# Decoder layer: the normalised tokens of the later batches rounded in two pairs, context queries rounded later, feed-forward seams rearranged

## The chip, the cores and the metric

The kernel runs as one program on one core of a Trainium2 chip. The core has a matrix engine (PE in the profile, with its weight loads as PEld), a vector engine (DVE), a scalar engine (ACT), GpSimd (POOL) and SP, which here only issues DMAs. Each engine takes its own instructions strictly in the order in which the program gives them, and waits where an operand is not there yet. The metric is the device time of one execution in microseconds, lower is better, as the median of several runs.

## The reference

One decoder layer over `x` of 8 batches, 112 tokens, 512 features, with a context of 375 tokens for each batch:

```python
x = x + attention(layernorm(x), Wqkv, Wqkv_b)              # 16 heads of 32, rotary, causal
# second attention, on l = _ln(layernorm(x), ln_w, ln_b):
q  = (_div_clamp_fp8(l, q_in_scale)  * q_in_scale)  @ wq   # and k, v with scales of their own
qx = (_div_clamp_fp8(l, qx_in_scale) * qx_in_scale) @ wqx  # queries of the context
core = gqa(ln(q), ln(k), v); xout = gqa(ln(qx), ln(kx), vx)  # kx, vx from ctx_2048
x = x + _div_clamp_fp8(concat(core, xout), proj_smooth) @ wproj * scale
# feed-forward with ternary weights
x = x + rms_norm(silu(gate) * up) @ ternary(w_proj),  gate, up = layernorm(x) @ ternary(w_gate_up)
```

`_div_clamp_fp8` divides by a scale, clips to 448 and rounds to an 8-bit float. The same normalised tokens are rounded four times, with four scales: m = 0 for q, 1 for k, 2 for v, 3 for the context's queries.

## The kernel before

The program is a hand-written order: the Python text runs once, and every call appends instructions to the engines' queues in that order. What is said here of order is therefore order on each engine. The stages, with their place in the profiled execution of before:

- **First attention.** Batches 0 to 3, then their transition, then batches 4 to 7 (from about 114 us). `batch(b, ...)` issues, for a pipeline of three batches, `values(b)`, `attended(b-2)`, `scores(b)`, `turned(b-1)` and `softmaxed(b)`. `joined` adds the result to `xb[b]` on POOL (L611), takes the statistics of `xb[b-1]` and normalises `xb[b-2]` on DVE (L161).
- **Rounding (`quantise`).** A group is a column block k of 128 features of four batches, that is 448 tokens. `quantise_turn` transposes it on PE (L332). `quantise_begin` scales it on ACT (L350) and takes |y| on ACT (L203). `round_a` clips both on DVE (L207, L208) and adds them on POOL (L210). The last subtraction writes `xq[m]` (L368), on POOL for batches 0 to 3 with m < 3, else on DVE. There are 8 groups and 4 values of m, so 32 such tiles, all 448 wide. The 16 tiles of batches 0 to 3 are begun beside first attention, and those of batches 4 to 7 only in the units that follow, by `quantise((4, 5, 3, 1, 1, 1, 1)[u.i])` after unit 0, 1, 2 and so on; m = 3 comes last.
- **Weights.** `split_chunk(s, what, k)` splits a weight chunk into two parts on ACT (L309) and DVE (L310); what = 0 is q's weights, 1 keys' and values', 2 the output's. The tiles for the parts come from a `Ring` of pools A, B and C; `load_raw` issues the next chunk's DMA on SP. The chunks (0, 0, k) and (0, 1, k) of the first head group are split after first attention.
- **Own units** 0 to 31 (from 164.2 us): four head groups s, in each 7 token tiles of 128 and one more step. `Own.project` makes q (8 matmuls at L691, 512 wide), then keys and values, statistics on DVE (L173, L174), and between them it calls `advance(stage, g)`, which lets earlier units take their next stage: normalising, transposing (`turn`, whose keys go through DVE at L833), scores, softmax, output. Unit i reads token tile i mod 8, so unit 3 is the first that needs tokens of batch 4.
- **Context units** 32 to 63 (from about 460 us) do the same against the context, with `xq[3]` as input of their queries.
- **Seam to the feed-forward** (about 1078 to 1122 us): the dictionary `between` puts `ffn_input(0)` (normalise four tiles, transpose, split), four `hidden_part` calls for the first 512 tokens and the last units' stages one after the other; `ffn_input(1)` for the other 384 tokens follows.
- **Feed-forward**: `hidden_part` multiplies by gate and up, `down` multiplies back. In the last `down` the row norm `rstd` comes from PE, DVE and POOL (L133), and then DVE does two operations for each of 7 tiles (L1414, L1415) before its DMA goes out.

## Time and profile before

| | us |
|---|---|
| median of 3 runs (lowest, highest) | 1285.07 (1284.45, 1289.41) |
| the profiled execution's own time | 1283.86 |
| its span, first to last instruction | 1282.1 |
| PE busy in the span | 1200.6 (94%) |
| DVE, ACT, POOL busy | 931.8, 815.8, 846.1 |
| first attention's batches 4 to 7, 116.0 to 164.2 | 48.2; DVE busy 46.56 |
| own units 0 to 3, 164.2 to 214.2 | 50.0; DVE busy 39.18, PE busy 33.89 |
| eight own units in the steady part, 317.34 to 384.64 | 67.3; DVE busy 56.42, PE busy 62.77 |
| seam, 1078.0 to 1122.2 | 44.2; PE busy 36.08 |

The profile is one execution. Busy time is the union of an engine's instructions; matmul ends are modelled, so a busy PE is not a PE at its peak. A group of instructions is told by line, engine and tile (output, then inputs), with its count, busy time, mean time of one and the idle time in front of it. In a timeline the two first columns are the start and the length, and a bracket gives the idle time before the instruction and the one whose end released it. "PEclk" is the clock that the matrix engine was granted, as a share of full speed.

### The profile page before, as it was taken

To read this page: it belongs to the slowest core of one execution; us is meant where nothing else is said; L and a number is where in the kernel's file an instruction comes from. 1 tells how busy PE (TensorE), PEld (TensorE's weight loads), DVE (VectorE), ACT (ScalarE), POOL (GpSimd) and SP (SyncE) were. 2 spreads that over 40 slices of the span, in tenths; PEclk is the share of its full clock that TensorE was granted. 3 is DMA by queue.
4 is the path that set the end of the run, shared out by engine and by line. 5 is a ranking of instruction groups with operands and counts; after the bars stand their busy time and mean duration, and the time that the engine had idled before them with its cause. 6 is when DMAs were issued, how large, how long until landed. Compare 5 with 4: busy or idle time off the path is not lost. (4 is left out here: it accounts for less than half of the span.)

```text
span 1282.1 us, 19634 instructions
## 1 busy us (share of the span) xinstructions
PE 1200.6 (94%) x6326; PEld 962.4 (75%) x6326; DVE 931.8 (73%) x2366; ACT 815.8 (64%) x2008; POOL 846.1 (66%) x938
## 2 busy tenths in 40 slices
PE   8997976889999889999999999999999998899998
PEld 5673765777888767888788778788777786687876
DVE  6647986887888866677776776677777775579864
ACT  2334676878687757667667767777667665456432
POOL 6657866687877756765767656667566655477762
PEclk9988886999999999999999999999999999999999
DMA  5001120213332354455554455554544440133201
GB/s 172 1 1 42 34 91 17 83 50 106 131 127 93 122 209 152 147 201 194 182 174 151 151 171 174 162 170 161 174 150 148 167 157 5 34 107 104 73 29 58
DMA packets 55511, 149.85 MB, mean 117 GB/s; under 512 B 6400, under 2 KB 15744, under 8 KB 55408
## 3 DMA queue, kind: packets, MB, share of 16 engines
q1 hardware_dynamic: 55408, 148.59, 35.3%
q8 instruction: 50, 0.82, 0.3%
q14 instruction: 53, 0.43, 0.1%
HBM read 120.18 MB, written 26.56 MB: 114 GB/s over the span
## 5 line engine op out<-in xcount | busy, mean ns | idle before, releaser
L912 PE MATMUL pa<-wx,ct 128*125 128x512 f32 x1152 | 289.4, 400 | 2.4 <-ACT wx L293 1.5
L912 PEld LDWEIGHTS pa<-wx,ct 128*125 128x125 f32 x1152 | 208.9, 186 | 51.2 <-ACT wx L293 1.9
L210 POOL TENSOR_TENSOR f8t<-y,big 128x512 f32<-128x512 bf16 (+1 forms) x88 | 107.4, 1224 | 140.2 <-DVE big L208 139.8
L738 POOL TENSOR_TENSOR p<-p,ri 112x448 f32<-112x448 f32 (+1 forms) x64 | 118.1, 1846 | 35.6 <-DVE ri L736 35.4
L923 DVE TENSOR_TENSOR kv<-kv,pa 125x512 f32<-125x512 f32 x96 | 65.9, 687 | 98.7 <-PE pa L912 52.2
L691 PE MATMUL pa<-hi,xq 128*128 128x512 f32 (+2 forms) x352 | 112.9, 345 | 11.0 <-DVE xq L368 9.2
L997 ACT ACTIVATE p<-ps,cmx 112x375 f32<-112x375 f32 x128 | 71.8, 574 | 75.5 <-DVE cmx L996 75.5
L1256 PE MATMUL pa<-h3T,wf 128*128 128x512 f32 (+1 forms) x512 | 110.0, 371 | 2.7 <-DVE sg L1266 2.7
L691 PE MATMUL pa<-lo,xq 128*128 128x512 f32 (+2 forms) x352 | 107.5, 331 | 0.9 <-DVE lo L310 0.9
L1256 PEld LDWEIGHTS pa<-h3T,wf 128*128 128x128 f32 x512 | 92.9, 188 | 14.9 <-DVE sg L1266 3.6
L174 DVE BATCH_NORM_AGGREGATE mv<-bst 128x2 f32<-128x6 f32 (+1 forms) x472 | 86.0, 182 | 16.3
L691 PE MATMUL ps<-hi,cq 128*128 128x512 f32 x224 | 90.8, 405 | 2.8 <-POOL cq L758 1.1
L730 ACT ACTIVATE qT<-ps,hln 128x448 f32<-128x448 f32 (+6 forms) x112 | 57.4, 567 | 56.1 <-PE ps L725 55.8
L691 PE MATMUL ps<-lo,cq 128*128 128x512 f32 x224 | 88.4, 395 | 0.0
L173 DVE BATCH_NORM_STATS2 bst<-pa 128x6 f32<-128x128 f32 x280 | 76.2, 272 | 16.2 <-PE pa L691 16.2
L988 PE MATMUL ps<-kT,qT 128*112 128x375 f32 x256 | 86.0, 478 | 0.5 <-ACT kT L974 0.5
L1158 POOL TENSOR_TENSOR th<-th,tw 128x512 bf16<-128x512 bf16 x48 | 59.1, 1231 | 40.1 <-DVE th L1150 40.1
L193 ACT ACTIVATE kv<-kv,ckvnm,ckvr 125x128 f32<-125x128 f32 x192 | 77.5, 491 | 6.2 <-POOL ckvnm L189 5.5
L691 PEld LDWEIGHTS pa<-hi,xq 128*128 128x128 f32 (+1 forms) x352 | 67.9, 193 | 17.3 <-DVE xq L368 10.7
L1021 PE MATMUL ps<-pT,kv 125*128 125x224 f32 x384 | 78.0, 353 | 0.0
L1021 PEld LDWEIGHTS ps<-pT,kv 125*128 125x128 f32 x384 | 72.6, 190 | 2.0
L691 PEld LDWEIGHTS pa<-lo,xq 128*128 128x128 f32 (+1 forms) x352 | 68.0, 193 | 7.4 <-DVE lo L310 3.8
(181 smaller groups left out, 3131.1 us busy)
## 6 DMA issues: line engine op xcount, KB each, us to landing
ct<-forms SPq DMA_DIRECT2D x84, 750.0 KB, 4.4
w<-in_wattn SPq DMA_DIRECT2D x96, 256.0 KB, 3.1
forms<-form SPq DMA_DIRECT2D x12, 750.0 KB, 4.7
forms<-ct SPq DMA_DIRECT2D x12, 750.0 KB, 5.1
tr<-in_wgu SPq DMA_DIRECT2D x32, 256.0 KB, 4.5
done<-th SPq DMA_DIRECT2D x48, 128.0 KB, 4.3
wh<-done SPq DMA_DIRECT2D x24, 256.0 KB, 3.7
tr<-in_wdown SPq DMA_DIRECT2D x16, 256.0 KB, 4.4
```

The lines of the kernel that those rows point to most:

```text
L173: nc.vector.bn_stats(st[: self.rows], a)
L174: nc.vector.bn_aggr(self.mv[: self.rows, self.at, :], st[: self.rows])
L193: nc.scalar.activation(dst, src, AF.Identity, bias=self.nm[:rows, i : i + 1], scale=self.r[:rows, i : i + 1])
L210: nc.gpsimd.tensor_tensor(t, y16, big, ALU.add)
L691: nc.tensor.matmul(out_, lhsT=lhsT, rhs=part[:, cut], start=first and i == 0, stop=last and i == 1)
L738: nc.gpsimd.tensor_tensor(u.p, u.p, bc, ALU.mult)
L912: nc.tensor.matmul(banks[bank][:CJ, :], lhsT=ct[:, at : at + CJ] if ct.dtype == F32R else ct[:, at : at + CJ].bitcast(F32R), rhs=split[sel ...
L923: nc.vector.tensor_tensor(kv, kv, banks[1][:CJ, :], ALU.add)
L988: nc.tensor.matmul(pp[:S, :SC], lhsT=qT[:, j, :], rhs=self.kT[:, j // 2, :], start=True, stop=True,)
L997: nc.scalar.activation(self.p[:, j, :], pp[:S, :SC], AF.Exp, bias=nm[:S], accum_out=self.sums[:S, j : j + 1])
L1021: nc.tensor.matmul(po[:, cut], lhsT=self.kv[j][:, 256 + g * P : 256 + (g + 1) * P], rhs=self.pT[:, j, cut], start=(j == 0), stop=(j == NJ ...
L1256: nc.tensor.matmul(pp[:, :n], lhsT=wcur[k][:, m * 256 + blk * P : m * 256 + (blk + 1) * P], rhs=hT[half, k][i], start=(k == 0 and i == 0), ...
```

## The change

- `qgroups` becomes (0, 1, 2, 3), (4, 5), (6, 7) by four values of k: the later batches are rounded in pairs, in tiles 224 wide. Each group has three rounded tiles (m = 0, 1, 2), 36 in all; for m = 3 only the scaled values are written to `xq[3]`, unrounded.
- `quantise` clips and subtracts one tile earlier than before, and now runs between batches, beside `batch(8)` and `batch(9)`, and, through `spot(i, n)`, at four places inside units 0 to 2 instead of after units.
- `round_q3` rounds `xq[3]` one token tile (128 partitions x 4 x 128) at a time inside units 5, 7, 9, 12, 14, 16 and 19.
- `joined` is only the addition; `normed` has the statistics (half 0) and the normalising (half 1).
- Pool `a1` moves to the other side of the memory, so that the weights' pool and ring B can open when the projections of first attention end; six of the first eight chunks are split inside the loop over batches 4 to 7, the other two beside `batch(8)` and `batch(9)`. Ring A has 16 tiles and A2 8 in place of 24.
- Seam: `ffn_input` is cut into `input_norms`, `input_turns` and `input_splits`, which are put between the last units' stages; the transposes go to `pa` banks (for the second half two `ps` and two `pa`).
- Last `down`: for tiles 3 to 6 the first of DVE's two operations becomes a scaling on ACT and an addition on POOL.

```diff
-    qgroups = [(0, k, (0, 1, 2, 3)) for k in range(KC)] + [(1, k, (0, 1, 2)) for k in range(KC)]
-    qgroups += [(1, k, (3,)) for k in range(KC)]
+    qgroups = [(bs, k) for bs in ((0, 1, 2, 3), (4, 5), (6, 7)) for k in range(KC)]
+    qtiles = [(i, m) for i in range(len(qgroups)) for m in range(3)]
...
+        scaled(y, i, m)
         qstate["y", t] = round_begin(y, s0, 6)
+        if m == 2:
+            k, cols = tokens_of(i)
+            scaled(xq[3][:, k, cols], i, 3)
...
-            if t < qstate["begun"] - (3 if begin else 0):
+            if t < qstate["begun"] - (2 if begin else 0):
...
-                engine = nc.vector if half or m == 3 else nc.gpsimd
+                engine = nc.vector if i >= KC else nc.gpsimd
...
+    def round_q3(b, step):
+        y = xq[3][:, :, b * P : (b + 1) * P]
+        if step == 0:
+            big = w2.tile([P, KC, P], BF, tag="f8m", name=uid("big"))
+            nc.scalar.activation(big, y, AF.Abs, scale=2.0**20)
+            q3state[b] = big
+        elif step == 1:
+            big = q3state[b]
+            nc.vector.tensor_scalar(y, y, 448.0, -448.0, ALU.min, ALU.max)
+            nc.vector.tensor_scalar(big, big, 448.0 * 2.0**20, 1.5 * 2.0**14, ALU.min, ALU.max)
+            t = w2.tile([P, KC, P], F32, tag="f8t", name=uid("f8t"))
+            nc.gpsimd.tensor_tensor(t, y, big, ALU.add)
+            q3state[b] = t, big
+        else:
+            nc.vector.tensor_tensor(y, *q3state.pop(b), ALU.subtract)
...
         for b in range(HB, B):
-            batch(b, B, 4 if b < B - 1 else 0)
-            quantise(4, False)
+            batch(b, B, 3 if b < B - 1 else 0)
+            quantise(3, False)
             if b >= HB + 2:
-                joined(b - 2, HB, B)
+                normed(b - 2)
+            for what, k in {HB: (), HB + 1: ((0, 0), (0, 1)), HB + 2: ((0, 2), (0, 3)), HB + 3: ((1, 0), (1, 1))}[b]:
+                split_chunk(0, what, k)
...
+    batch(B, B)
+    quantise(3, False)
+    split_chunk(0, 1, 2)
+    normed(B - 2, 0)
+    quantise(2)
+    normed(B - 2, 1)
+    to_tiles(B - 2)
+    quantise(2)
+    batch(B + 1, B)
+    split_chunk(0, 1, 3)
+    normed(B - 1, 0)
+    quantise(2)
+    normed(B - 1, 1)
+    quantise(2)
+    to_tiles(B - 1)
...
+    begins = {0: (1, 1, 1, 1), 1: (2, 2, 2, 2), 2: (2, 2, 0, 0)}
+    rounds = dict(zip((5, 7, 9, 12, 14, 16, 19), range(NT)))
+    def spot(i, n):
+        if i in begins:
+            quantise(begins[i][n])
+            if i == 2 and n > 1:
+                quantise(4, False)
+        elif i in rounds and n != 1:
+            round_q3(rounds[i], (0, None, 1, 2)[n])
...
-        if u.i < 7:
-            quantise((4, 5, 3, 1, 1, 1, 1)[u.i])
-        if u.i in (2, 7, 8):
-            quantise(5 if u.i == 2 else 3, False)
...
+    input_norms(0, 1)
+    last(1, "normed", "weigh")
+    input_norms(2, 3)
+    last(1, "out")
+    input_turns(0, 0, 1, 2, 3)
+    last(1, "turn_p", "attend", "turn", "rounded")
+    input_splits(0)
+    last(1, "score")
+    hidden_part(0, 0, 0)
+    last(2, "weigh")
+    hidden_part(0, 1, 0)
+    last(2, "turn_p", "out", "attend")
+    input_norms(4, 5)
+    last(2, "rounded")
+    hidden_part(1, 0, 0)
+    input_turns(1, 4, 5)
+    last(3, "out")
+    input_norms(6)
+    hidden_part(1, 1, 0)
...
+                for i in range(3, NT):
+                    nc.scalar.activation(ys[i], ys[i], AF.Copy, scale=rstd[:, i : i + 1])
+                    nc.gpsimd.tensor_tensor(ys[i], ys[i], xs[i], ALU.add)
...
-                nc.vector.scalar_tensor_tensor(ys[i], ys[i], r, xs[i], ALU.mult, ALU.add)
+                if i < 3:
+                    nc.vector.scalar_tensor_tensor(ys[i], ys[i], r, xs[i], ALU.mult, ALU.add)
```

`spot(i, 0)` stands after q's statistics of unit i, 1 before its keys and values, 2 after `advance("attend")` and before `advance("turn")`, 3 at the unit's end. `last(n, ...)` runs the named stages for the units that are left.

## The prediction

> **What bounds the kernel now.** I read the page first, then PE's busy time in short stretches, then what PE waited for, then the places where it waited, in order of time. The page says that PE is busy 94% of the span:
>
> ```profile
> PE 1200.6 (94%) x6326; PEld 962.4 (75%) x6326; DVE 931.8 (73%) x2366; ACT 815.8 (64%) x2008; POOL 846.1 (66%) x938
> ```
>
> So PE bounds the kernel, and what this change can win is PE's 81.5 us of idle time, or part of it. Busy time per stretch (columns: stretch, its length, then busy time and count for PE, PEld, DVE, ACT, POOL, then granted clock, DMA share, GB/s) shows the worst place:
>
> ```profile
> 184.00:188.00 4.00, 2.75 (x25) 2.53 (x23) 2.91 (x6) 2.52 (x5) 3.75 (x4) 1.00 0.00 0
> 188.00:192.00 4.00, 0.74 (x3) 0.41 (x3) 3.86 (x14) 3.61 (x8) 2.55 (x2) 0.91 0.00 0
> 192.00:196.00 4.00, 3.96 (x13) 2.54 (x12) 2.62 (x11) 4.00 (x15) 2.85 (x5) 0.50 0.00 0
> 196.00:200.00 4.00, 0.00 (x0) 0.00 (x0) 2.03 (x7) 1.13 (x3) 4.00 (x4) 0.50 0.00 0
> 200.00:204.00 4.00, 1.22 (x2) 0.50 (x2) 4.00 (x6) 3.94 (x10) 2.76 (x3) 0.50 0.00 0
> 204.00:208.00 4.00, 1.59 (x6) 1.38 (x7) 4.00 (x7) 0.46 (x2) 2.56 (x2) 0.50 0.00 0
> ```
>
> Of these 24 us PE is idle 13.74 (24 minus the sum of its column). That is unit 3, and the list of PE's waits names the tile, the rounded tokens of batches 4 to 7 that are not written yet (columns: total us, times, longest):
>
> ```profile
> PE pa L691 <- DVE xq L368: 9.2, 2, 6.1
> PE ps L332 <- DVE h L161: 6.8, 5, 3.2
> PE ps L725 <- ACT q L193: 4.5, 1, 4.5
> ```
>
> What makes the rounding late is DVE. In 116.0 to 214.2 (batches 4 to 7 and units 0 to 3) it is busy 46.56 + 39.18 = 85.7 of 98.2 us, 87%. Its groups there, by shape:
>
> ```profile
> L207 DVE TENSOR_SCALAR y<-y 128x448 bf16<-128x448 bf16 x28 | 16.1, 574 | 0.8 <-ACT big L203 0.8
> L208 DVE TENSOR_SCALAR big<-big 128x448 bf16<-128x448 bf16 x28 | 11.8, 421 | 0.0
> L368 DVE TENSOR_TENSOR xq<-f8t,big 128x448 fp32r<-128x448 f32 x12 | 10.7, 904 | 3.1 <-POOL f8t L210 3.1
> L368 DVE TENSOR_TENSOR xq<-f8t,big 128x448 bf16<-128x448 f32 x4 | 3.3, 825 | 0.0
> ```
>
> The reader is to see that 27.9 + 14.0 = 41.9 us, half of DVE's work there, is rounding. The other two places are the seam to the feed-forward, where PE's order shows its waits in brackets, and the tail:
>
> ```profile
> 1082.77 1.56 PE L1009 MATMUL ps<-ident,p 112*125 112x112 f32 x12 [2.54 <-POOL p L738]
> 1091.79 2.96 PE L1227 MATMUL ps<-ident,h 128*128 128x128 f32 x16 [1.14 <-ACT p L997]
> 1112.66 0.50 PE L691 MATMUL ps<-hi,cq 128*128 128x512 f32 x1 [1.12 <-POOL cq L758]
> 1120.03 0.30 PE L1227 MATMUL ps<-ident,h 128*128 128x128 f32 x1 [1.64 <-DVE h L161]
> ...
> 1266.70 9.58 PE L1389 MATMUL ps<-wf,hid 128*128 128x512 f32 x40
> 1267.12 1.52 POOL L133 TENSOR_TENSOR rms<-rms,expo 128x7 f32<-128x7 f32 x1 [2.25 <-DVE rms L1409]
> 1278.47 0.75 DVE L1415 SCALAR_TENSOR_TENSOR y<-ps,rms,y 128x512 f32<-128x512 f32 x1
> ```
>
> At the end PE is done at 1276.28 and DVE at 1279.22, so the last 3 us are DVE's.
>
> **Part 1, the rounding up to unit 4.** Before, 28 tiles are clipped in the stretch (0.574 + 0.421 = 0.995 us each) and 16 subtracted on DVE, 41.9 us. After, 12 tiles of 448 (11.9 us of clips, their subtraction on POOL, no m = 3) and 24 tiles of 224. The trace has no 224-wide rounding. Its two bounds are half of a 448 tile, (0.995 + 0.904) / 2 = 0.95 us, and a whole one, 1.90. I take half, because the nearest narrow row is near it: DVE's 112x256 multiplication at L547 takes 0.424 us where the 448-wide one at L508 takes 0.625, and without POOL at work the clips at 182.60 and 182.78 take 0.27. So 11.9 + 24 x 0.95 = 34.7 us, 7.2 less; with whole tiles 57.5 us, 15.6 more.
>
> The six weight chunks that move into the loop cost DVE the same as before (2.7 + 3.3 us at L310 for all eight, in this stretch in both kernels), and ACT 2.6 + 3.3 us. Their 13 loads go to SP earlier, ahead of the copies of x to its tiles; these are first read by the output of unit 5, over 30 us later, and the DMA share in 120 to 160 is under 0.2, so I cost them at nothing; without that cover a load costs the 3.1 us that it takes to land.
>
> `normed(4)` and `normed(5)` now stand in the loop: DVE's L161 waits for two small POOL instructions (0.25 and 0.55 us) queued behind up to three additions and three subtractions, 3 x (1.167 + 1.081) = 6.7 us at worst. Behind L161 on DVE stand the chunk splits and the next batch's values, on which PE waits. The row for it is 0.7 us (the one such wait in this stretch). I do not price it alone: I keep DVE's busy share at 87%, which leaves 11.5 us for waits of this kind.
>
> ACT gains the narrow tiles: 12 x 1.30 + 24 x 0.65 and eleven to twelve unrounded scalings of 0.36 to 0.72 make some 37 us where 31.2 were, on 63.4 busy of 98.2; it stays below DVE. POOL (70.0 us busy) loses about 4.
>
> So the stretch becomes (85.7 - 7.2) / 0.873 = 89.9 us against 98.2: **8.3 us won**. The bounds: at whole-tile price (85.7 + 15.6) / 0.873 = 116.0, 17.8 lost; with PE's own busy time of the stretch as floor (45.48 + 33.89 = 79.4), 18.8 won. Where does the stall go? To units 0 to 2, which carry 16 of the narrow tiles and will show short waits for statistics and keys; by unit 2's end all is written, before unit 3 reads it.
>
> [...]
>
> The granted clock is 0.70 on average in 164.2 to 214.2 (0.50 in four of the rows above), and PE is busy 33.89 us there. [...] I take nothing, as these matmuls run while DVE is behind.
>
> **Part 2, the context's queries.** Units 4 to 11 take 70.25 us (214.20 to 284.45), the steady eight 67.30. The difference of 2.95 is the four m = 3 tiles that are finished in bunches after units 7 and 8: unit 9's q starts at 255.68 and unit 10's 11.57 later, where 8.3 is usual. That goes. Instead seven units get 1.4 us of DVE (two clips of 0.28, a subtraction of 0.83), 1.2 of POOL and 0.65 of ACT. The cover is DVE's idle time, 67.3 - 56.42 = 10.9 us in eight units; the two clips stand ahead of the keys' move (L833), for which PE already waits 7.4 us in six places. Bounds: nothing, or 7 x (1.61 + 0.28) = 13.2 if each clip meets POOL (L207 in the steady stretch takes 1608 ns on average). I take 1 us in all, since units 4 to 7 of before held a 448 tile each and took 8.1 us against 8.4 in the steady part. **2 us won.**
>
> **Part 3, the seam.** PE idles 2.54 + 0.49 + 1.14 + 0.18 + 1.12 + 1.64 + 0.36 = 7.47 us between 1078.15 and 1122.21. After: the 16 input transposes (2.96 us) fill the wait of 2.54 for p, since the rows of tiles 0 to 3 are complete by 1070.6. The scores and the splits (four at 0.62) let the first hidden part begin at about 1090.9. A new wait: p of the last unit needs its reciprocal on DVE, which now stands behind the first hidden part's multiplication, which waits for Silu, which waits for the exponentials and a table load of 1.28 us. Silu ends at 1096.5, multiplication 1097.2, reciprocal 1097.4, POOL's 2.69 us 1100.1, while PE is through with the second hidden part at 1098.4: 1.7 us idle. Another: the second half's first hidden part takes a `pa` bank that holds transposes until its split is done, three of four splits at 0.4 to 0.5 us after the last transposes, 1.9 us. I count 7.47 - 1.7 - 1.9 - 0.6 for the small ones left = **3.3 us won**; bounds 0 (as many waits as before) and 6.
>
> **Part 4, the tail.** Seven pairs take DVE from 1268.67 to 1279.22. After: three pairs to 1273.1; ACT's scaling (0.6) and POOL's additions (1.3 each) give tiles 3 to 6 at 1270.6, 1271.9, 1273.2 and 1274.5, in time; the last waits for PE's end at 1276.28 and is done at 1277.15. **2.1 us won**; bounds 1.5 and 2.2, as nothing else stands behind.
>
> **Sum.** 8.3 + 2.0 + 3.3 + 2.1 = 15.7 us. The profiled execution took 1283.86 us, its span 1282.1 and 1.8 around it; the span should become 1266.4. The median of the runs is 1.2 above the profiled time: 1285.07 - 15.7 = 1269.4.
>
> **Rivals.** (a) The stall is only spread: units 0 to 2 lengthen by what unit 3 loses, because DVE's clips wait on POOL (L207 takes 1.10 us beside an addition at 188.52, 0.27 alone). For it: in 184 to 208 DVE and POOL take turns, one tile in 1.74 us. Against it: PE has a unit of slack before it needs the tiles. Part 1 wins nothing: 1285.07 - 7.4 = 1277.7. (b) PE becomes the only bound, part 1 wins 18.8: 1258.9; the transposes and the work of units 0 to 2 before pipelines are full speak against it. (c) Slower: a narrow tile costs DVE as much as a wide one, 1.90 us, at the clips and subtractions of units 0 to 2 and ahead of unit 0. Part 1 loses 17.8 and the rest wins 7.4: 1295.5. It decides from a loss of 7.4 us in part 1 on, that is 24 tiles at (41.9 + 0.873 x 7.4 - 11.9) / 24 = 1.52 us each. For it: the turn-taking of 1.74 us; against it: L547 against L508. (d) The seam does not fill, as its new waits equal the old: 1272.7; that is within the first case's range.
>
> **How the numbers follow.** Forecast with (d): 0.56. (a): 0.20. (b): 0.12. (c): 0.12. The time is the first's, 1269.4; its own range is 1263 to 1276. The range reaches into (a) and most of the way to (b), 1260 to 1281, and leaves out about 2 in 10. A measurement of this kernel tells 0.5% from no change, that is 1278.6. Faster: the first, (b) and half of (a), 0.77; same: the other half of (a) and a little of (c), 0.13; slower: 0.10.
>
> **What would show it.** Right: no wait of L691 for the rounded tokens at unit 3, unit 4's q at about 206; 224-wide clips and subtractions of some 0.95 us a tile; eight units from unit 4 in 68 us; the second half's first hidden part at about 3 us less behind the last context unit; DVE's last operation within 1 us of PE's end. Wrong: units 0 to 2 that take longer by what unit 3 saves, or DVE at 1.5 us a narrow tile, or loop batches of 13 us.

## The result and the profile after

The changed kernel takes 1293.50 us (median of 7 runs, 1291.02 to 1295.38), where the kernel before takes 1285.07 (7 runs beside them, 1282.16 to 1289.41). The ratio is 1.0061, 95% interval 1.0045 to 1.0078: slower by 0.6%, just above what a measurement of this kernel can tell from no change. The forecast was 1269.4, faster by 15.7 us.

The profiled execution took 1293.82 us, its span is 1292.0, 9.9 more than before. The starts of PE's steps in the two timelines, cut into stages, show where (us; "first attention" begins with the first matmul of softmax weights by values, "unit 0" is the start of its q):

| stage | before | after | difference | forecast |
|---|---|---|---|---|
| start to first attention | 54.32 | 58.23 | +3.9 | 0 |
| first attention to unit 0 | 109.88 | 116.60 | +6.7 | |
| unit 0 to unit 8 | 82.43 | 81.63 | -0.8 | -8.3 with the row above |
| unit 8 to unit 32 | 213.05 | 219.68 | +6.6 | -2.0 |
| unit 32 to the end | 822.42 | 815.86 | -6.6 | -5.4 |

The last row came about as forecast. The two parts that round tokens both went the other way. (The 3.9 us of the first row are taken up below: they are not the change's.)

PE is still the engine with the most work, but it now waits more. The page's line of busy times, and then the list of PE's waits (total us, times, longest):

```profile
PE 1204.4 (93%) x6310; PEld 965.6 (75%) x6310; DVE 933.2 (72%) x2395; ACT 823.1 (64%) x2039; POOL 849.5 (66%) x953
```

```profile
PE ps L883 <- DVE kT L875: 15.9, 10, 6.1
PE ps L870 <- DVE x L753: 9.3, 9, 1.7
PE ps L1051 <- POOL p L778: 6.3, 10, 1.9
PE ps L765 <- ACT q L193: 4.6, 1, 4.6
...
PE ps L546 <- DVE v L487: 3.0, 1, 3.0
```

The 9.2 us for the rounded tokens, first in the list of before, are gone, as forecast. The keys' wait has grown from 7.4 to 15.9 (L833 is now L875), and the wait for the output's addition into x (L753) from 3.4 to 9.3. The last line is new. Its place, in order of time (start, length, engine, line; in brackets the idle time and its releaser):

```profile
148.65 1.03 POOL L377 TENSOR_TENSOR xq<-f8t,big 128x448 fp32r<-128x448 f32 x1
149.76 1.03 POOL L210 TENSOR_TENSOR f8t<-y,big 128x448 f32<-128x448 bf16 x1
150.76 1.03 POOL L377 TENSOR_TENSOR xq<-f8t,big 128x448 fp32r<-128x448 f32 x1
151.86 1.03 POOL L210 TENSOR_TENSOR f8t<-y,big 128x448 f32<-128x448 bf16 x1
152.85 1.03 POOL L377 TENSOR_TENSOR xq<-f8t,big 128x448 fp32r<-128x448 f32 x1
153.97 0.19 POOL L154 TENSOR_SCALAR lr<-lmv 112x1 f32<-112x1 f32 x1
154.24 0.55 POOL L133 TENSOR_TENSOR lr<-lr,expo 112x1 f32<-112x1 f32 x1
154.82 0.55 DVE L161 TENSOR_SCALAR h<-xb,lmv,lr 112x512 f32<-112x512 f32 x1 [6.21 <-POOL lr L133]
155.28 1.41 DVE L310 SCALAR_TENSOR_TENSOR lo<-w,vec,hi 128x512 fp32r<-128x512 f32 x2
156.61 0.69 DVE L487 TENSOR_TENSOR v<-ps,vb 112x512 f32<-112x512 f32 x1
157.35 1.74 PE L546 MATMUL ps<-ident,p 112*112 112x112 f32 x8 [3.00 <-DVE v L487]
158.88 6.05 PE L562 MATMUL ps<-v,pt 112*112 112x33 f32 x32
```

Read it downwards. POOL's lr for batch 4 needs 0.74 us, but stands behind five additions and subtractions of the rounding. DVE waits 6.21 us for it at the normalisation. Behind that stand two weight splits and the values of batch 7, whose bank PE needs: PE waits 3.00. Then the attention of batch 6 takes 6.05 us where the same 32 matmuls took 3.68 before (154.94 to 158.62, at a granted clock of 1.00). The next two rows are windows (window, length, then busy time and count of PE, PEld, DVE, ACT and POOL, granted clock, DMA share, GB/s); the first shows the granted clock of the changed kernel, 0.50, and the second is the stretch over which the prediction reckoned:

```profile
160.00:180.00 20.00, 20.00 (x97) 18.72 (x97) 15.14 (x41) 13.06 (x31) 8.96 (x13) 0.50 0.48 144
...
116.08:222.89 106.81, 85.15 (x535) 68.57 (x534) 76.67 (x227) 70.97 (x164) 61.70 (x83) 0.76 0.16 50
```

In the second row DVE is busy 76.67 of 106.81 us, 72%, where it was 87%. DVE's own list of waits in 120 to 225 says for what:

```profile
DVE xq L377 <- POOL f8t L210: 10.1, 7, 3.4
DVE h L161 <- POOL lr L133: 8.1, 3, 6.2
```

In the units, the rounding of the context's queries shows in DVE's waits from unit 4 to 32, and at one of its places in the timeline:

```profile
DVE xq L397 <- POOL f8t L394: 9.3, 4, 2.7
```

```profile
278.79 1.75 DVE L397 TENSOR_TENSOR xq<-f8t,big 128x512 bf16<-128x512 f32 x1 [2.70 <-POOL f8t L394]
```

The seam and the tail, where the prediction was right (PE's waits in brackets, and the last instruction of DVE):

```profile
1099.30 0.66 PE L1288 MATMUL pa<-ident,h 128*128 128x128 f32 x4 [1.66 <-DVE h L161]
...
1116.75 1.56 PE L1051 MATMUL ps<-ident,p 112*125 112x112 f32 x12 [1.92 <-POOL p L778]
...
1278.74 9.56 PE L1466 MATMUL ps<-wf,hid 128*128 128x512 f32 x40
...
1288.41 0.75 DVE L1496 SCALAR_TENSOR_TENSOR y<-ps,rms,y 128x512 f32<-128x512 f32 x1 [0.52 <-PE ps L1466]
```

The predicted wait of 1.7 us for p is there, 1.92; the first line is a wait of 1.66 that was not named; and DVE's last operation waits for PE alone.

### The profile page after: what moved, and what is told of

Read it like the earlier page. It is cut to its first block, busy times and chain, and to the rows that moved or that the text cites. A ratio compares the mean times of both kernels' runs of the same rounds, so it can differ in the third digit from the quotient of the medians.

```text
span 1292.0 us, 19686 instructions
## 1 busy us (share of the span) xinstructions
PE 1204.4 (93%) x6310; PEld 965.6 (75%) x6310; DVE 933.2 (72%) x2395; ACT 823.1 (64%) x2039; POOL 849.5 (66%) x953
## 5 line engine op out<-in xcount | busy, mean ns | idle before, releaser
L210 POOL TENSOR_TENSOR f8t<-y,big 128x512 f32<-128x512 bf16 (+2 forms) x92 | 98.7, 1076 | 145.8 <-DVE big L208 145.3
L1323 PEld LDWEIGHTS pa<-h3T,wf 128*128 128x128 f32 x512 | 93.0, 188 | 15.9 <-DVE sg L1333 3.6
L770 ACT ACTIVATE qT<-ps,hln 128x448 f32<-128x448 f32 (+6 forms) x112 | 57.3, 566 | 54.3 <-PE ps L765 54.3
```

Of the source, the lines that this page charges most:

```text
L210: nc.gpsimd.tensor_tensor(t, y16, big, ALU.add)
L1323: nc.tensor.matmul(pp[:, :n], lhsT=wcur[k][:, m * 256 + blk * P : m * 256 + (blk + 1) * P], rhs=hT[half, k][i], start=(k == 0 and i == 0), ...
```

## The experiments

All stages below are read from one profile of each kernel, as in the table above; ratios are to the kernel before, timed on the same chip. The stage sums of one profile vary by some microseconds from execution to execution, as the two profiles of the changed kernel show.

| run | first attention to unit 0 | to unit 8 | to unit 32 | to the end | time, us | ratio, 95% interval |
|---|---|---|---|---|---|---|
| before | 109.9 | 82.4 | 213.1 | 822.4 | 1285.07 | |
| changed | 116.6 | 81.6 | 219.7 | 815.9 | 1293.50 | 1.0061 (1.0045, 1.0078) |
| after_again | 120.3 | 81.9 | 219.8 | 816.2 | 1290.57 | 1.0043 (1.0027, 1.0058) |
| seam_tail | 107.9 | 82.0 | 213.1 | 817.1 | 1279.25 | 0.9961 (0.9940, 0.9983) |
| norm_first | 113.6 | 81.9 | 221.3 | 816.7 | 1290.41 | 1.0033 (1.0017, 1.0048) |
| no_q3 | 115.1 | 80.8 | 210.3 | 816.0 | 1280.49 | 0.9955 (0.9939, 0.9971) |
| deeper | 115.0 | 81.0 | 219.8 | 816.6 | 1290.89 | 1.0047 (1.0030, 1.0064) |
| q3_pool | 113.6 | 82.4 | 217.6 | 818.4 | 1288.85 | 1.0027 (1.0011, 1.0043) |
| q3_late | 113.4 | 81.6 | 212.2 | 818.5 | 1283.82 | 0.9989 (0.9973, 1.0006) |
| warm | 118.1 | 81.8 | 219.7 | 816.3 | 1293.54 | 1.0060 (1.0037, 1.0083) |
| splits_late | 106.8 | 86.5 | 219.7 | 817.2 | 1287.31 | 1.0020 (1.0002, 1.0038) |
| units_end | 108.7 | 85.3 | 213.0 | 816.4 | 1280.06 | 0.9951 (0.9934, 0.9968) |
| units_warm | 112.1 | 86.3 | 213.1 | 817.2 | 1280.63 | 0.9959 (0.9943, 0.9975) |
| best | 106.0 | 83.1 | 211.8 | 817.0 | 1274.19 | 0.9910 (0.9890, 0.9930) |
| best_pairs | 103.6 | 84.6 | 214.8 | 816.5 | 1279.61 | 0.9963 (0.9943, 0.9984) |
| best_spots | 104.7 | 82.6 | 212.8 | 818.7 | 1274.48 | 0.9926 (0.9905, 0.9946) |
| best_now | 106.2 | 83.2 | 219.7 | 818.4 | 1282.31 | 0.9978 (0.9963, 0.9993) |
| best_joins | 115.6 | 82.6 | 210.6 | 818.1 | 1283.02 | 0.9999 (0.9977, 1.0020) |

**Seam and tail alone (seam_tail).** The kernel before with the diff's last parts, from `input_norms` on, and nothing else.

> The kernel before with only the new seam to the feed-forward and the new tail. Theory: these two are independent of the rounding and win what the trace of the changed kernel shows for them, 4.6 + 2.1 = 6.7 us: 1278.4 us. Rival: the seam's gain hangs on the state in which the changed kernel arrives there (other banks, the clock), then 1281 to 1283.

5.3 us were won behind unit 32 on the profile (822.4 against 817.1), 5.2 in the times (1279.25 against 1284.43 for the kernel before beside it). This is a little under the 6.7, and not the rival: the two parts stand on their own, and make a kernel that is faster than both.

**The changed kernel once more (after_again).**

> The changed kernel unchanged, for a second profile beside the same runs of the kernel before. In its first profile the granted clock falls to 0.50 for 6.4 us from 26.5 us on, and first attention's first attention matmul comes 2 to 3.6 us later than in every other profile, before anything that the change could have moved. If that is chance: the first attention matmul at 54.5 to 56.5 us, unit 0 at 169.5 to 171.5, units 8 to 32 219.7 us as before, and the profiled time 1289 to 1292. If it belongs to the change: 58 us again, unit 0 at 174 to 175, and 1293 to 1295.

Half of each. First attention's first matmul is at 54.84 us, so the 3.9 us of the first row of the table were chance, as the same kernel has them once and once not: in 5 of the 18 profiles of this study the granted clock falls to 0.50 for 3.4 to 6.8 us at 26 us, and these five are the ones that reach first attention at 55.9 to 58.2 us; the other 13 reach it at 54.3 to 55.5. (All five are kernels that round in pairs; eight profiles of such kernels, after_again among them, and the five of kernels that don't, pass the place at 1.00.) But the stage behind it took 3.7 us more, and unit 0 is at 175.09 again. A single profile up to unit 0 is thus good to some 4 us.

**The order of lr and rounding on POOL (norm_first).**

```diff
             batch(b, B, 3 if b < B - 1 else 0)
-            quantise(3, False)
             if b >= HB + 2:
-                normed(b - 2)
+                normed(b - 2, 0)
+            quantise(3, False)
+            if b >= HB + 2:
+                normed(b - 2, 1)
```

> The changed kernel, with the statistics of the joined batch put ahead of the rounding's additions and subtractions on POOL in the loop over batches 4 to 7, and its normalisation behind them. Theory: DVE's 6.2 us wait for POOL's lr, the 3.0 us that PE waits behind it, and the 24 us at a granted clock of 0.50 that follow all go; unit 0's q starts some 7 to 10 us earlier (165 to 168 us on its profile), and the time is 1284 to 1287. Rival: the clock is low because the batches at the end of first attention feed PE with small matmuls and wait on ACT and DVE anyway, then unit 0 stays within 2 us of 174.8 and the time at 1292.

DVE's wait for lr in 120 to 170 fell from 7.2 us in the changed kernel to this:

```profile
DVE h L161 <- POOL lr L133: 1.9, 2, 1.0
```

Unit 0 came at 168.6. But the kernels no_q3 and deeper, which still have the wait in the loop, have it at 170.1 and 169.6. By the stage up to unit 0, the three profiles with norm_first's first part (norm_first, q3_pool, q3_late) have 113.4 to 113.6 us, the three with the changed kernel's (changed, after_again, no_q3) 115.1 to 120.3. The times (1.0033 against 1.0061 and 1.0043) overlap with the changed kernel's. The wait went, PE's gap of 3.0 us shrank to 1.25, and most of the loss stayed, the low clock with it: it fell to 0.50 at 145 us and stayed there up to unit 0. So the theory that wait, gap and low clock go together was half right at best. The early splits are still in the loop in this run; the next run takes them out.

**The early splits (splits_late).** norm_first, without `split_chunk` in the loop; the eight chunks are split behind batch 8 and batch 9.

```diff
-            for what, k in {HB: (), HB + 1: ((0, 0), (0, 1)), HB + 2: ((0, 2), (0, 3)), HB + 3: ((1, 0), (1, 1))}[b]:
-                split_chunk(0, what, k)
...
-    split_chunk(0, 1, 2)
+    for k in range(KC):
+        split_chunk(0, 0, k)
...
-    split_chunk(0, 1, 3)
+    for k in range(KC):
+        split_chunk(0, 1, k)
```

> As the run norm_first, with the first eight weight chunks split where the kernel before does it, after the loop over the batches. Theory: the early splits win nothing, since they are hidden behind PE's work at the end of first attention, and cost some of DVE's time behind which PE waits for a bank in the loop; unit 0 starts at 165 to 168 us and the time is 1287 to 1291. Rival: they are needed there, unit 0 waits for the chunks and starts at 170 to 174.

The stage up to unit 0 fell from 113.6 to 106.8 us (units_end, with the same first part, has 108.7). So the early splits cost 6.8 us there, or 5 to 7 by all five profiles, which the prediction had counted at nothing. A part of it goes with the clock: the attention of batch 6 takes 6.04 us in norm_first, at 0.50, and 3.63 here. Of the 6.8 us, 4.6 are given back between units 0 and 8, where PE now waits 1.9 us for normalised tokens and 1.2 us more for q (6.6 against 5.4). By the ratios 1.7 us are left in the times, less than the intervals can tell.

**The granted clock (warm).** norm_first, with the mask's four matmuls done three times in batches 4 to 7, and 16 more ahead of each of the last two attentions.

```diff
+            elif last == B:
+                warm = pa()
+                for _ in range(16):
+                    nc.tensor.matmul(
+                        warm[:S, :SH],
+                        lhsT=identr,
+                        rhs=maskr.rearrange("p (o t) -> p o t", o=1).to_broadcast([S, 4, S]),
+                        start=True,
+                        stop=True,
+                    )
```

> As the run norm_first, with idle matmuls added: the mask's four matmuls are done three times in each of batches 4 to 7 (8 x 0.26 us more a batch), and 16 more of them go into a free bank ahead of the attention of batches 6 and 7. Theory: from 145 us to unit 0 the granted clock is 0.50 because PE's work there (33 to 112 columns a matmul) is too thin to keep or to regain the full clock; with the dense ones the clock comes back before 160, the attentions L562 of batches 6 and 7 take 3.3 instead of 6.0 us, and unit 0 starts 1 to 5 us earlier than 168.6, in spite of some 6 us of added matmuls at the end. Rival: the clock follows PE's idle gaps, and the added matmuls only add their time: attentions at 6.0 us, unit 0 at 172 to 178.

PE's timeline:

```profile
153.91 3.48 PE L660 MATMUL pa<-maskr,identr 112*112 112x448 f32 x16 [0.62 <-DVE p L534]
157.23 3.24 PE L562 MATMUL ps<-v,pt 112*112 112x33 f32 x32
...
164.26 5.29 PE L660 MATMUL pa<-maskr,identr 112*112 112x448 f32 x16
169.39 3.24 PE L562 MATMUL ps<-v,pt 112*112 112x33 f32 x32
```

With the added matmuls the clock stayed at 1.00 up to 161 us, and both attentions took 3.24 us in place of 6.04. But they cost more than they returned: the stage up to unit 0 is 4.6 us longer than in norm_first, and the time is the changed kernel's. In units_warm, a smaller dose, unit 0 again came later:

> As units_end, with fewer idle matmuls than in the run warm: eight more of the mask's in batch 7 (2.1 us) and eight in a free bank ahead of the attention of batch 6 (2 us). Theory: these are enough to hold the clock at 1.00 to the end of first attention, which returns 2 x 2.8 us in the two attentions and 1.7 in the transposes between them: unit 0 starts 1 to 4 us earlier than in units_end. Rival: the added time eats it, unit 0 is within 1 us or later.

The stage up to unit 0 took 112.1 us against 108.7, and the times are equal. So the low clock is a part of the loss, 2 x 2.8 = 5.6 us in two attentions against warm's 3.24 at a clock of 1.00 and 4.8 against the kernel before (3.68 and 3.64 there), but filling PE is no remedy.

**The rounding of the later batches (deeper, units_end).** In deeper the pipeline is as long as before; in units_end (on splits_late) the tiles are begun four at a time behind units 0 to 3, with the late subtraction of q3_late below.

```diff
-            if t < qstate["begun"] - (2 if begin else 0):
+            if t < qstate["begun"] - (3 if begin else 0):
...
-            if left > (1 if begin else 2) or (left and not begin and qstate["clipped"] == qstate["begun"]):
+            if left > 2 or (left and not begin and qstate["clipped"] == qstate["begun"]):
```

> The changed kernel with the rounding's pipeline as deep as before: a tile is clipped three tiles after it is begun and subtracted when more than two are clipped, where the change made it two and one. Theory: in units 0 to 3 DVE's subtraction waits for the addition on POOL issued just before (10.1 us in 7 waits); with one more tile between them that falls to some 3 us, and unit 0 to unit 4 take 48.1 - 4 to 7 = 41 to 44 us; 1286 to 1290 us. Rival: DVE and POOL are the limit by their busy time there, so the wait only moves elsewhere and unit 0 to 4 stay at 47 to 49 us, 1292 to 1294.

DVE's wait L377 for L210 from unit 0 to 4 fell from 9.6 to 2.6 us, and unit 0 to 4 took 47.4 us against 48.1. The rival is right about the units: the wait moved to others. (The time, 1290.89, lies between the two ranges.)

> As the run splits_late, with two more edits: round_q3's subtraction in the next unit as in q3_late, and the later batches' rounding begun four tiles at a time at the ends of units 0 to 3 and finished at the end of unit 4, where the changed kernel puts it between the steps of units 0 to 2. Theory: inside a unit the clips, additions and scalings stand ahead of the unit's own statistics, powers and keys on DVE, POOL and ACT, and PE waits 5 to 7 us a time for these (q 6.6, kT 7.3 us in splits_late); at the units' ends, and over five units, most of these waits go: unit 0 to unit 4 take 40 to 46 us where splits_late has 52.9, and with the 6 us of q3_late the time is 1270 to 1275. Rival: the rounding's total work on DVE and POOL is the limit up to unit 4, wherever it is put; then 50 to 53 us, and 1279 to 1282.

Unit 0 to 4 took 42.5 us, as the theory had it, and units 4 to 8 then 42.8, where splits_late has 33.5. Up to unit 8 it is 85.3 against 86.5. The time is the rival's, although units 8 to 32 are 6.7 us shorter, by the late subtraction.

**The context's queries (no_q3, q3_pool, q3_late, best_now).** no_q3 is the changed kernel with `round_q3` left out, so that the context's queries stay unrounded. q3_pool and q3_late are norm_first with another place for its last step, the subtraction: q3_pool puts it on POOL. q3_late puts it into the next unit, behind that unit's statistics, scores and output:

```diff
-        elif i in rounds and n != 1:
-            round_q3(rounds[i], (0, None, 1, 2)[n])
+        elif i in rounds and n in (0, 2):
+            round_q3(rounds[i], n // 2)
+        elif i - 1 in rounds and n == 1:
+            round_q3(rounds[i - 1], 2)
```

> The changed kernel without the rounding of the context queries' input: xq[3] stays scaled and unrounded, so the seven times five instructions of round_q3 are left out. Theory: these are what lengthens units 4 to 23, then units 4 to 32 take 253.3 - 8 to 10 = 243 to 245 us and the time is 1284 to 1286. Rival: the pipeline runs in another phase since unit 4 (units 17, 18 and 20 are long without any rounding in them), then units 4 to 32 take 250 to 253 us and the time is 1290 to 1293.

> The changed kernel with the earlier normalisation of the run norm_first, and with round_q3's subtraction on POOL, right behind its addition, in place of DVE. Theory: the rounding costs 10 us in units 4 to 32 not by DVE's work (1.4 us a unit) but because DVE's subtraction waits for POOL's addition, which stands behind POOL's powers and p, and the next unit's statistics and the output's addition into x stand behind the subtraction; on POOL there is no such wait, and units 4 to 32 take 255.7 - 6 to 9 = 247 to 250 us, the time 1281 to 1285. Rival: any engine's extra work delays the units, POOL's 1.2 us a unit then costs what DVE's did: 253 to 257 us, 1288 to 1292.

> As the run norm_first, and round_q3's subtraction stays on DVE, but is issued in the next unit, behind that unit's statistics of q, scores and output. DVE's work is the same. Theory (the wait for POOL is the cost, and what stands behind it): units 4 to 32 take 247 to 250 us and the time is 1281 to 1285. Rival (DVE's added work is the cost): 253 to 256 us, 1288 to 1291.

Units 4 to 32 took 243.0 us without the rounding, 252.5 with the subtraction on POOL, 246.3 with it on DVE but later, and 255.7 in norm_first. The theory of q3_late holds: the same work on the same engine costs 9.3 us less when DVE doesn't have to wait for it (3.3 us are left, against no rounding at all). That of q3_pool doesn't: on POOL it is only 3.2 us better, and the time, 1288.85, is its rival's. That the subtraction then delays POOL's own powers and p, which stand behind it, would explain this, but is not shown.

**A better version (best), and parts of the change put back into it.** best is seam_tail, with three rounded tiles for each of the two wide groups, and the context's queries rounded as in q3_late. Everything else of the first part is as before the change.

```diff
-    qgroups = [(0, k, (0, 1, 2, 3)) for k in range(KC)] + [(1, k, (0, 1, 2)) for k in range(KC)]
-    qgroups += [(1, k, (3,)) for k in range(KC)]
+    qgroups = [(half, k, (0, 1, 2)) for half in range(2) for k in range(KC)]
...
+        if m == 2:
+            at = slice(12 + k, 13 + k)
+            q3 = xq[3][:, k, half * SH : (half + 1) * SH]
+            nc.scalar.activation(q3, qstate["ln"], AF.Identity, bias=lnb[:, at], scale=lnw[:, at])
```

> The run seam_tail, and from the change only the later rounding of the context's queries, with its subtraction in the next unit as in q3_late: the two halves stay wide (448 tokens), with three rounded tiles a group in place of four; splits, joins and statistics stay where the kernel before has them. Theory: what lost time in the first part are the pairs, the early splits and the statistics in the loop, and what lost time in the second part is only the place of the subtraction. So unit 8 starts 0 to 5 us earlier than in seam_tail (8 of 32 wide tiles of m = 3 are gone from DVE and POOL up to there), units 8 to 32 take 212 us where seam_tail has 213, and the time is 1273 to 1279. Rival: m = 3 was hidden in seam_tail, then the time is seam_tail's 1278 to 1280.

1274.19 us, ratio 0.9910 (0.9890 to 0.9930): faster than both kernels. It is the theory's number. Against seam_tail the profile has 0.8 us less up to unit 8 (189.1 to 189.9) and 1.2 less in units 8 to 32; the times have 5.1 less. The rest lies in which execution was profiled: seam_tail's took 1277.05 us, 2.2 less than the median of its runs (1276.45 to 1283.80), best's 1274.84, 0.7 more than its median. Where seam_tail's slower executions lose their time, no profile shows. best still has the stall of unit 3: PE waits 8.3 us there for rounded tokens.

best_now is best with `round_q3`'s subtraction put back where the changed kernel has it.

> The run best with round_q3's subtraction back at the end of its own unit, as the changed kernel has it. Theory: DVE waits there for POOL's addition, and the next unit stands behind it: units 8 to 32 take 219 to 221 us where best has 211.8, and the time is 1280 to 1284. Rival: the loss came with the state in which the changed kernel's units arrived, then units 8 to 32 take 212 to 214 us and the time is 1274 to 1276.

This is the clean one: the two kernels' units start within 0.1 us of each other up to unit 9 (254.12 and 254.22), and by unit 32 (456.11 and 464.11) best_now is 8.0 behind; in the times 8.1. DVE's waits from 200 to 460 us, first of best, then of best_now:

```profile
DVE bst L173 <- PE pa L713: 15.7, 12, 2.6
...
DVE xq L393 <- POOL f8t L390: 0.4, 1, 0.4
```

```profile
DVE bst L173 <- PE pa L713: 11.5, 8, 2.6
DVE xq L393 <- POOL f8t L390: 9.3, 4, 2.7
```

In best DVE waits for PE (the engine that bounds), in best_now for POOL. One place in best_now's timeline shows what POOL is busy with and what stands behind DVE:

```profile
262.87 0.28 DVE L387 TENSOR_SCALAR xq<-xq 128x512 bf16<-128x512 bf16 x1
262.89 1.48 POOL L133 TENSOR_TENSOR ownr<-ownr,expo 128x6 f32<-128x6 f32 x1
...
264.61 0.93 POOL L760 TENSOR_TENSOR p<-p,ri 112x448 f32<-112x448 f32 x1
265.50 1.16 POOL L390 TENSOR_TENSOR f8t<-xq,big 128x512 f32<-128x512 bf16 x1
266.62 1.29 POOL L301 TENSOR_TENSOR lo<-w,hi 128x512 fp32r<-128x512 f32 x1
266.69 1.76 DVE L393 TENSOR_TENSOR xq<-f8t,big 128x512 bf16<-128x512 f32 x1 [2.69 <-POOL f8t L390]
...
270.91 0.74 DVE L735 SCALAR_TENSOR_TENSOR x<-ps,psc,x 128x512 f32<-128x512 f32 x1
...
271.70 0.44 PE L854 MATMUL ps<-ident,k 128*128 128x128 f32 x2 [0.93 <-DVE x L735]
```

The clips are done at 263.4 and DVE's work behind them at 264.0; the addition waits behind powers and p to 265.50; DVE stands idle for 2.69 us, up to 266.69, and four microseconds later PE waits for the bank that DVE's addition into x (L735) has not emptied.

> The run best with its wide rounding tiles put inside units 0 to 2, at the four places where the changed kernel has them (4, 5 and 3 tiles), in place of the units' ends. Theory: a tile's clips, addition and scaling then stand ahead of the unit's own statistics, powers and keys on three engines in turn, and unit 8 starts 3 to 6 us later than in best: 1277 to 1281. Rival: the rounding's work up to unit 8 is the same wherever it stands: within 1.5 us of best.

best_spots puts best's wide tiles inside units 0 to 2: `quantise(((1, 1, 1, 1), (1, 1, 2, 1), (1, 1, 1, 0))[i][n])` in `spot`, and nothing behind the units. The rival is right, 1274.48 us: the place inside the units costs nothing.

> The run best with the later four batches rounded in two pairs, in tiles 224 wide, at the same places (8, 10 and 6 tiles after units 0, 1 and 2). Theory: the narrow tiles cost their price alone, DVE 1.03 us a tile where half a wide one is some 0.95, so 24 x 0.1 = 2 us on DVE, and one more hand-over between DVE and POOL for each of 12 more tiles; unit 8 starts 2 to 5 us later than in best and the time is 1276 to 1279. Rival: the tiles are no part of it, the pairs as such are harmless, then within 1.5 us of best (1273 to 1276).

best_pairs rounds the second half in pairs, with the changed kernel's `qgroups` and `scaled`, at best's places. The medians say 5.4 us more, the ratios (0.9963 against 0.9910) 6.8, just over the theory's upper end; the span says 2.5, and not where the theory has it: up to unit 8 the stages are 1.0 us shorter than in best, and 3.0 us are lost in units 8 to 32, where both kernels issue the same instructions. More than half of the 3.0 is lost between the q of unit 8 and that of unit 9, at a granted clock of 0.85 against 1.00. Both kernels have the same 51 matmuls there and the same two waits of PE (0.56 and 1.09 us), first best_pairs, then best:

```profile
244.25:255.72 11.47, 9.81 (x51) 7.88 (x50) 9.64 (x28) 6.86 (x20) 4.69 (x5) 0.85 0.30 91
```

```profile
244.28:254.12 9.84, 8.19 (x51) 6.52 (x50) 9.54 (x28) 6.82 (x20) 4.72 (x5) 1.00 0.34 107
```

And the profiled execution of best_pairs, 1277.37 us, is 2.2 below the median of its runs (1275.35 to 1284.08). The price is measured; its mechanism is not shown.

> The run best_pairs, and of the changed kernel's order in first attention one more part: the addition into x right behind each batch's attention, and the statistics and the normalisation of batches 4 to 7 one and two batches earlier than before (batches 4 and 5 in the loop, behind the rounding as in the changed kernel). Splits stay late, the rounding starts after unit 0. Theory: DVE waits in the loop for POOL's lr, behind the rounding's additions and subtractions (6.2 us in the changed kernel), and the next batches' work stands behind it: the stretch from the first attention matmul to unit 0 takes 103.6 us in best_pairs and 106 to 110 here, unit 8 is 2 to 5 us later and the time is 1281 to 1285. Rival: without the early splits behind it the wait costs nothing, within 1.5 us at unit 8: 1278 to 1281.

best_joins is best_pairs with the changed kernel's joins:

```diff
                 attended(b - 2, va.pop(b - 2), pt.pop(b - 2))
+                if last == B:
+                    nc.gpsimd.tensor_tensor(xb[b - 2], xb[b - 2], outs.pop(b - 2), ALU.add)
...
-                joined(b - 2, HB, B)
+                normed(b - 2)
```

The attention of batch 5 starts at 143.92 us here and at 143.99 in best_pairs, so from there on the two can be laid side by side. Unit 0 then starts 10.2 us later (169.90 against 159.66), unit 8 8.2 and unit 32 4.0 later; the ratios say 0.9999 against 0.9963, some 4.6 us, the medians 3.4, and the two intervals just touch. The theory holds, up to unit 8 beyond its upper end. In best_joins:

```profile
149.31 1.03 POOL L377 TENSOR_TENSOR xq<-f8t,big 128x448 fp32r<-128x448 f32 x1
150.42 0.19 POOL L154 TENSOR_SCALAR lr<-lmv 112x1 f32<-112x1 f32 x1
150.69 0.55 POOL L133 TENSOR_TENSOR lr<-lr,expo 112x1 f32<-112x1 f32 x1
151.28 0.55 DVE L161 TENSOR_SCALAR h<-xb,lmv,lr 112x512 f32<-112x512 f32 x1 [4.21 <-POOL lr L133]
152.57 2.29 PE L546 MATMUL ps<-ident,p 112*112 112x112 f32 x12 [3.02 <-DVE ari L572]
...
154.66 6.05 PE L562 MATMUL ps<-v,pt 112*112 112x33 f32 x32
```

and in best_pairs the same two steps of PE:

```profile
149.02 1.75 PE L546 MATMUL ps<-ident,p 112*112 112x112 f32 x16
150.60 3.68 PE L562 MATMUL ps<-v,pt 112*112 112x33 f32 x32
```

The granted clock, over the same four microseconds of best_pairs and of best_joins:

```profile
156.00:160.00 4.00, 3.95 (x38) 3.76 (x37) 3.81 (x7) 3.42 (x6) 2.04 (x3) 1.00 0.56 148
```

```profile
156.00:160.00 4.00, 4.00 (x24) 4.00 (x23) 3.05 (x6) 1.72 (x3) 1.58 (x3) 0.50 0.54 147
```

One wait of DVE for a 0.74 us pair of instructions on POOL makes a 3.0 us gap on PE, and 0.6 us behind the gap the clock is halved for all that is left of first attention. That the gap took the clock is the order of events in this profile and not more: in the changed kernel's profile the clock fell at 149.5 us and in after_again at 150.4, 4 to 5 us ahead of the gap of 3 us. PE looks as busy in the second row, and does less: 24 matmuls in place of 38.

With the joins, best_joins needs 198.2 us from first attention to unit 8, as much as the changed kernel (198.2 and 202.1 in its two profiles), without the early splits: the prices of the parts do not add up. Its time with best_now's 8.1 us on top is 1291.1, where the changed kernel took 1293.50 and 1290.57.

## Why the prediction was wrong

**Where it failed first: "I do not price it alone: I keep DVE's busy share at 87%, which leaves 11.5 us for waits of this kind."** The prediction had found the wait of L161 for lr, had its worst case (6.7 us; it was 6.21), and had named what stands behind it. It then folded it into a share measured on a kernel where such a wait was 0.7 us. DVE's work in the stretch did fall as reckoned, from 85.7 to 76.7 us (7.2 were forecast, it was 9.1), and a narrow tile cost 1.03 us where 0.95 was taken (clips 0.306 and 0.226, subtraction 0.499, in 116 to 225 us of the changed kernel), 24 x 0.08 = 1.9 us in all. But the busy share went from 87% to 72%, and time is work divided by share. Put back alone, the joins cost 10.2 us at unit 0, 8.2 at unit 8 and 3.4 to 4.6 in the times.

**The splits: "their 13 loads go to SP earlier ... I cost them at nothing".** No wait for a load shows in 116 to 175 us of the changed kernel's profile. The term that was missing is the splits' place on DVE and ACT: at the end of first attention they were hidden behind PE's own work, in the loop they stand ahead of the next batch. That is 6.8 us at unit 0, 2.2 at unit 8.

**The clock: "I take nothing, as these matmuls run while DVE is behind."** Not asked was whether the change could lower the clock where PE does set the pace. In the last two batches the clock was lower: 0.50 from 156.3 to 180.2 us, where before has 1.00 in 144 to 163. Each attention took 6.05 us in place of 3.68 and 3.64 before, the transposes between them 3.39 in place of 1.99. The joins (best_joins) and the early splits (norm_first against splits_late) each bring a longer low clock; what in them takes it stays open.

**Where does the stall go?** The prediction let unit 3's stall of 13.74 us become "short waits". In every run the stretch from unit 0 to unit 8 takes 81 to 87 us, the kernel before included (82.4). In units 0 to 3 of before PE waits 9.2 us for rounded tokens, 4.5 for q and 2.4 for normalised tokens, 16.1 in all; in the changed kernel 4.6 for q at 190, and then

```profile
195.22 0.63 PE L331 MATMUL ps<-ident,h 112*128 112x112 f32 x2 [2.77 <-ACT xq L341]
201.61 0.60 PE L331 MATMUL ps<-ident,h 112*128 112x112 f32 x2 [2.31 <-DVE kT L875]
216.04 1.81 PE L883 MATMUL ps<-kT,qT 128*112 128x112 f32 x8 [6.12 <-DVE kT L875]
```

which makes 15.8 in all: the stall for the tokens became one behind other work of DVE and ACT, the keys above all. In splits_late, where unit 0 comes earlier (106.8 us), the stretch is longer (86.5), and in units_end, where units 0 to 4 are quicker, units 4 to 8 are slower. Rival (a), a stall that is only spread, was right about what comes of this stretch; it had 0.20.

**Part 2: "I take 1 us in all, since units 4 to 7 of before held a 448 tile each ..."** 8.0 us (best_now against best). The bound of 13.2 held it; its mechanism did not: it was reckoned from clips that meet POOL, and the clips took 0.28. The row used for the 1 us was a kernel whose rounding stood behind whole units, with its subtraction two tiles behind its addition. Here the subtraction stood directly behind an addition on POOL that is itself queued. L397 should have had a price of its own: POOL's powers, p and addition (1.48 + 0.93 + 1.16 us in the rows above) against what DVE has left to do. With the late subtraction the gain of the bunched tiles that part 2 forecast shows: 212 us against 213 in units 8 to 32, 1 us where 2 were forecast.

**Parts 3 and 4** were right: 6.6 us from unit 32 on in the profile, 5.4 forecast; the tail's 2.1 us to the tenth, the seam some 4.5 where 3.3 were forecast, with the wait of 1.7 us for p at its place (1.92); the 1.9 for the `pa` bank came as twice 0.24, and one of 1.66 for a normalised tile was not foreseen.

**Rival (c)**, the slower case, had the sign and 0.12, with the wrong mechanism, so that it would have been right by luck: narrow tiles were not dear on DVE (1.03 us each, where it took 1.90). The true slower case, a wait of DVE on POOL in the loop with PE's clock behind it, was in the text and had no chance of its own. (The prediction's parts of "faster" add up to 0.78, where it says 0.77.)

What stays open: why pairs cost some 5 us in the times when the profile of best_pairs is ahead of best up to unit 8; what makes the clock fall in the last batches; and how much of the changed kernel's loss up to unit 0 is the rounding begun beside batches 8 and 9 or the new places of the memory pools, which no run had alone.

## What to carry to other kernels

When an edit puts an instruction that waits for another engine into the middle of a queue, price that one wait: the other engine's queue ahead of the releaser, less what the waiter still has to do, and then whatever stands behind the waiter. A busy share from the old kernel doesn't contain it. The same work, moved a few steps later in its own queue, so that the releaser has been served by then, can cost much less: here DVE's 9.3 us of waiting became 0.4, and the kernel 8 us faster. And work that is hidden where it stands (the splits) is not free where it is moved to.

## What the runs showed of the hardware

- PE's clock stayed low where PE's records show it busy. In best_joins it was 0.50 up to unit 0 (153.2 to 169.9), with PE busy 16.68 of the 16.70 us, all in matmuls with 33 and 112 columns. With 16 matmuls of 448 columns ahead of each attention (warm) it was 1.00 in both attentions (3.24 us each), and 0.50 for some 7 us between them (the second 16 matmuls took 5.29 us, the first 3.48).
- What takes the clock is not shown. In best_joins it fell 0.6 us behind a gap of 3.0 us on PE (149.55 to 152.57); in norm_first it fell at 145 us with no gap over 1.6 us in the 16 us before. In the changed kernel it fell at 149.5 us, with no gap on PE since one of 1.57 us that ended at 140.92; from 152.9 to 156.3 it was 1.00 again, though PE was busy for only 0.7 of the 3 us from 153 to 156.
- The clock's falls did not repeat from profile to profile: five of 18 profiles lose it at 26 us, as told above, and 13 pass the same place at 1.00; the changed kernel has done both, in one profile each; best_pairs loses it in unit 8, where best, with the same matmuls and waits, keeps it.
- The same row lasted longer beside some rows of the other engine. In before a clip of 448 columns on DVE (L207) took 1.10 us at 188.52, beside POOL's addition L210 (188.21 to 189.49), and 0.27 at 182.60; there POOL was at work too, which the prediction denies, but on its power of 128 x 6 (L133, 182.43 to 183.79). POOL's L154 on 112 x 1 took 0.19 us at 160.44 and 2.90 at 162.62, beside four weight splits of DVE (L310, 2.73 us in a row). The changed kernel's subtraction L397 on DVE took 0.68 us at 244.39, with POOL idle, and 1.75 at 278.79, beside POOL's L301 (1.28 us from 278.72); best's took 0.68 in the median and 2.55 at most. What lengthens these rows is not shown.
